# Layer 0 of a four-layer Flamingo stack: rope of the context in place on VectorE, attention in nine turns, routing in twelve parts

## The chip, the cores and the metric

The kernel runs on one core of a Trainium2 chip. The metric is the device time of one execution in microseconds (us); lower is better. A core has a TensorE (PE in the profile), a VectorE (DVE), a ScalarE (ACT), a GpSimd (POOL) and a SyncE (SP), which here only issues transfers. All of them run their own instructions in order and wait for each other through semaphores; 16 DMA engines move data.

## The reference, cut to what matters

There are 16 sequences of 56 tokens of width 256 (896 tokens), and for each a context of 1500 rows of width 64. Four layers follow each other, each a gated cross attention and a gated feed-forward part, both on the normalised x and added to x:

```python
# layer 0: x is (16, 56, 256), ctx is (16, 1500, 64)
x = x + tanh(g_xattn[0]) * mha(norm(x), ctx)   # 16 heads of 16; token i sees the context's rows 0 to i, so 56 at most
x = x + tanh(g_ffn[0])   * moe(norm(x))        # 16 routed experts, top 4, and 2 shared experts
# layers 1 to 3: attention over all 1500 rows of the context
#   keys  = ctx * cos + rotate_half(ctx) * sin            # "rope", the same for each of the three layers
#   x = x + tanh(g) * attention(norm(x), keys); then a matrix in fp8 (layer 1) or routed experts (2, 3)
```

The rope of the context (16 x 1500 x 64 numbers) depends on nothing that layer 0 makes. It is needed first by layer 1's attention.

## The kernel before, in words

The 896 tokens are eight tiles of 112 (`NT`, two sequences each). `x` stays in SBUF for the whole kernel, and so does `kv`, the roped context: 125 partitions, for each of the eight tiles 12 rows of the context x 2 sequences x 64 per partition. Layer 1 reads `kv` when it turns it into its keys.

Nearly every instruction is recorded with `in_order`, which keeps the order of the program on its engine. So the order that the code writes down is the order on each engine's queue, and a wait holds up all that stands behind it on that engine.

Layer 0's attention is `attention_mha`. First x, weights and the first 56 context rows (`k0`) are loaded, x is normalised (`norm`, L470 to L474), turned and multiplied with the query weights (L482 to L498). Then a loop of ten turns (`for i in range(NT + 2)`) works on three tiles at once. In turn i, tile i gets its scores (TensorE, L509 and L515), the shift by the row's maximum (VectorE, L529 and L530) and the exponential (ScalarE, L533); the weights of tile i-1 are turned (L540, L542), multiplied with the values (L549) and divided (L557, L558); and tile i-2's context is turned (L563, L565), projected (L570) and added to x (L573). At a turn's end the next tile's keys (L449, copied by ScalarE at L452 into `kb`) and values (L458, copied at L463 into `vb`) are made.

Between these steps `route(i, phase)` advances the routing. `Router.token_tiles` is a generator for a batch of two tiles: statistics (L1034), the inverse root (L131 to L141), the normalised rows (L1040), their transposes (L1048) and the product with the router weights (L1056), softmax (L1059 to L1065), the rank of every expert by comparing all pairs (L1069 to L1073), the choice and running totals (L1074 to L1081), the rows' places (L1091 to L1102), and eight indirect transfers by POOL that scatter the rows into `rows` in DRAM (L1106). Its `yield`s cut it into nine parts. Two of the four batches are left over at the loop's end; `moe` finishes them (`before`, `last`), and writes the table of tiles (`r.table()`) and the first products of the shared experts (`now`, L1414, then L1425 to L1433) between them.

`rows` must be cleared ahead of the scatters: `clear_rows` issues 16 transfers of zeros from SP (L1162).

Rope is the class `Roping`. `load` brings one tile's context from DRAM into `raw` (two buffers, SP, L874), and `parts` makes the rope on GpSimd: raw times cos into `kv` (L880), then for each half raw times sin into `rot` and an addition (L885, L886). Tiles 0 to 3 are roped in the first four turns, tiles 4 to 7 in parts between the routed tiles; the loads of tiles 6 and 7 are issued when these begin.

The routed tiles (`tiles` in `moe`) are 34 tiles of up to 128 rows of one expert, with nine spare ones that run only when needed. For each, SP loads weights and rows three tiles ahead (L1197, L1198, L1204); TensorE turns the rows (L1211), multiplies (L1223), turns the product (L1234) and multiplies again (L1245); ScalarE has the activation (L1227), VectorE the multiplication with it (`act`, L1228), a copy (`hT`, L1236) and the addresses (`to`, L1215); POOL scatters the result (L1248). `during(i)` adds work after each tile: the second half of the shared experts after every fourth, rope after every second.

Of the kernel before, what the change touches and what calls it, by code (L numbers as in the profile page):

```python
# [36 lines left out]
F32 = mybir.dt.float32  # L37
# [9 lines left out]
L, DC = 1500, 64  # L47
# [27 lines left out]
def flamingo_kernel(ctx: ExitStack, tc: tile.TileContext, d: dict, out: bass.AP):  # L75
# [72 lines left out]
    def inverse_root_now(pool, var, n):  # L148
        root = inverse_root(pool, var, n)
        while True:  # L150
            try:
                next(root)
            except StopIteration as e:
                return e.value
# [225 lines left out]
    def attention_mha(router, roping):  # L380
        with ExitStack() as st:
# [18 lines left out]
            def load_k0(b, queue):  # L400
                in_order(queue.dma_start(k0[S * b : S * b + S], d["ctx"][:, 0:S, :].rearrange("(t b) s c -> b s t c", b=2)[b]))
# [12 lines left out]
            kb = ap1.tile([128, 4, 2, 4, S], F32, name="kb")  # L414
# [6 lines left out]
            in_order(nc.gpsimd.memset(kb, 0.0))  # L421
            in_order(nc.gpsimd.tensor_copy(identb, ident))
            in_order(nc.gpsimd.tensor_copy(maskb, bcast(mask, 1, 8)))
            in_order(nc.gpsimd.memset(qT[:, :, B * S :], 0.0))

# [5 lines left out]
            for t in range(2):  # L431
                roping.load(t, nc.sync)
# [12 lines left out]

            def keys(t):
                ps = ps_k.tile([128, 512], F32, name="k_ps")[:, 0 : 4 * TP].rearrange("p (q n) -> p q n", q=4)
                for q in range(4):
                    in_order(nc.tensor.matmul(ps[:, q, :], wk[:, q, :], k0d[:, 2 * t : 2 * t + 2, 0, :], start=True, stop=True))  # L449
                for h in range(4):  # L450
                    i = ps[32 * h : 32 * h + 32].rearrange("p q (b s) -> p q b s", b=2)
                    in_order(nc.scalar.copy(kb[32 * h : 32 * h + 32, :, :, h, :], i))  # L452

            def make_values(t):
                vb = vbs[t % 2]
# [5 lines left out]
                pv = ps.rearrange("p (b g a c) -> p b g a c", b=2, g=H // 2, a=2)  # L461
                for a in range(2):
                    in_order(nc.scalar.activation(vb[:, :, :, 16 * a : 16 * a + 16], pv[:, :, :, a, :], AF.Copy, scale=small[0:TP, C_M + a : C_M + a + 1]))  # L463
                return vb
# [35 lines left out]
            class Pair:  # L500
# [3 lines left out]
                def scores(self):  # L504
                    t = self.t
                    self.s = []
                    for u in range(2):
# [4 lines left out]
                        for q in (2 * u, 2 * u + 1):  # L512
                            for b in range(2):
# [4 lines left out]
                                    kb[:, q, b].rearrange("p h s -> p (h s)"),  # L518
# [16 lines left out]
                def turned(self):  # L535
                    self.pT = ap.tile([TP, H // 2, 128], F32, name="pT0")
                    for u in range(2):
# [3 lines left out]
                        copy = nc.scalar.copy if u == 0 else nc.vector.tensor_copy  # L541
                        in_order(copy(self.pT[:, 4 * u : 4 * u + 4, :], ps))  # L542

                def values(self):

                    self.c = misc()
                    for g in range(H // 2):
                        for b in range(2):
                            in_order(nc.tensor.matmul(  # L549
                                self.c[64 * b : 64 * b + 64, 34 * g : 34 * g + 34], self.pT[:, g, 64 * b : 64 * b + 64], self.vb[:, b, g], start=True, stop=True  # L550
# [28 lines left out]
            def route(i, phase):  # L579

                k = i - 4 - "abc".index(phase)
                if k >= 0 and k % 2 == 0 and k // 2 < len(batches):
                    next(batches[k // 2])
# [7 lines left out]
            pairs[0].vb = make_values(0)  # L591
            norm(0)
            turn_normed(0)
            queries(0)
            norm(1)
            in_order(nc.scalar.activation(gates, gates, AF.Tanh))
            for i in range(NT + 2):
                new, turn, last = at(i), at(i - 1), at(i - 2)
                if turn:
                    turn.turned()  # L600
                if last:
                    last.turn_context()
                route(i, "a")
                if new:
                    new.scores()
                route(i, "b")
                route(i, "c")
# [3 lines left out]
                route(i, "b")  # L611
                if turn:
                    turn.values()
                if last:
                    last.project()
                if turn:
                    turn.normalize()
                if last:
                    last.add()
# [3 lines left out]
                if i + 1 < NT:  # L623
                    keys(i + 1)
                    pairs[i + 1].vb = make_values(i + 1)
                route(i, "c")
                route(i, "a")
                route(i, "b")
                route(i, "a")
                route(i, "b")  # L630
                if i < 4:
                    roping.rope(i)
                    roping.load(i + 2, nc.sync)
                    for _ in range(5):
                        next(clear, None)
# [227 lines left out]
    class Roping:  # L863
        def __init__(self, pool):
            self.pool, self.raw = pool, {}
            self.cos = pool.tile([KP, KC, DC], F32, name="cos")
            self.sin = pool.tile([KP, KC, DC], F32, name="sin")

        def load(self, t, queue, pool=None):
            if t == 0:  # L870
                in_order(queue.dma_start(self.cos, d["cos_k"]))
                in_order(queue.dma_start(self.sin, d["sin_k"]))
            self.raw[t] = (pool or self.pool).tile([KP, 2, KC, DC], F32, name="raw", bufs=2)
            in_order(queue.dma_start(self.raw[t], d["ctx"][2 * t : 2 * t + 2].rearrange("b (p c) e -> p b c e", c=KC)))  # L874

        def parts(self, t):
            hd = DC // 2
            raw = self.raw.pop(t)
            o = kv[:, t].rearrange("p c b e -> p b c e")
            in_order(nc.gpsimd.tensor_tensor(o, raw, bcast(self.cos, 1, 2), ALU.mult))  # L880
            yield
            for h in range(2):
# [837 lines left out]
```

## Time and profile before

| | |
|---|---|
| time, median of 3 runs | 2383.44 us (2382.97 to 2384.99) |
| profiled execution: time, span | 2402.98 us, 2401.2 us |
| TensorE, VectorE, ScalarE, GpSimd busy | 94%, 64%, 51%, 17% of the span |
| attention's first scores (L509) | start at 22.32 us |
| turned weights of tiles 0, 1, 2 (L540) | start at 34.97, 41.45, 49.10 us |
| last addition of attention (L573) | starts at 140.65 us |
| first rows of routed tiles turned (L1211) | starts at 183.83 us |
| layer 1's attention, first steps on POOL (L746) | starts at 393.41 us |

A line of a view in order of time has the start, the length, engine, line of the kernel, operation, output and inputs, shapes, and in brackets how long the engine sat idle before it and who ended that wait. L703 is line 703 of the kernel; DMA in brackets is a transfer. POOL and SP show the issue of a transfer, not its length.

### The profile page before, as it was taken

What the parts mean: (1) busy time and instruction counts of PE and PEld (TensorE: products, weight loads), DVE (VectorE), ACT (ScalarE), POOL (GpSimd) and SP (SyncE); (2) the same over time, 40 slices, a digit from 0 to 9 for tenths busy, and PEclk for the clock granted to TensorE, in tenths of its full rate; (3) what the DMA queues carried; (4) which work ended last, traced back from release to release, by engine and by line L of the source; (5) the groups of instructions that cost most, each with busy time, mean ns of one, the idle gap of its engine ahead of it and who ended that gap; (6) DMA issues with size and microseconds to landing.
All of it is one profiled execution on the core that took longest, in us unless ns stands there. A gap on an engine that the chain in (4) does not pass through costs nothing. (4 is left out here: it accounts for less than half of the span.)

```text
span 2401.2 us, 47945 instructions
## 1 busy us (share of the span) xinstructions
PE 2248.3 (94%) x17853; PEld 1613.1 (67%) x17858; DVE 1532.0 (64%) x3546; ACT 1232.0 (51%) x2703; POOL 416.3 (17%) x715
## 2 busy tenths in 40 slices
PE   8668889999999999999999999979899999999697
PEld 5445665777777775447777777745577777777454
DVE  4752245778777777667777777624577777776222
ACT  4312335666666663346666666513566666665131
POOL 5445710000000002420000000001001111101233
PEclk9769999999999999989999999989899999999799
DMA  7726762000000002200000000054101000000596
GB/s 217 225 80 184 215 169 78 22 21 22 21 22 21 21 24 68 61 21 22 23 24 21 13 23 24 10 200 157 32 22 30 29 30 16 28 24 21 153 284 206
DMA packets 116676, 172.98 MB, mean 72 GB/s; under 512 B 20154, under 2 KB 78531, under 8 KB 115412
## 3 DMA queue, kind: packets, MB, share of 16 engines
q1 hardware_dynamic: 106902, 151.35, 20.9%
q0 software_dynamic: 7600, 17.14, 2.2%
q8 instruction: 144, 2.36, 0.4%
q10 hardware_dynamic: 1934, 1.34, 0.2%
q14 instruction: 96, 0.79, 0.1%
HBM read 131.24 MB, written 40.48 MB: 72 GB/s over the span
## 5 line engine op out<-in xcount | busy, mean ns | idle before, releaser
L726 ACT ACTIVATE p<-s_ps,nm 128x500 f32<-128x500 f32 x504 | 335.7, 675 | 364.7 <-DVE nm L717 364.7
L703 PE MATMUL s_ps<-kvT,qT 64*128 64x500 f32 x2016 | 487.5, 610 | 9.9 <-ACT p L735 4.1
L777 PEld LDWEIGHTS m_ps<-pT,kv 125*64 125x64 f32 x8064 | 436.7, 137 | 65.8 <-issue 57.1
L777 PE MATMUL m_ps<-pT,kv 125*64 125x128 f32 x8064 | 477.3, 275 | 1.8 <-ACT pT L770 1.2
L715 DVE TENSOR_REDUCE part<-s_ps 128x1 f32<-128x500 f32 x504 | 340.6, 678 | 216.3 <-PE s_ps L703 215.9
L703 PEld LDWEIGHTS s_ps<-kvT,qT 64*128 64x128 f32 x2016 | 186.7, 190 | 198.1 <-issue 123.8
L765 PE MATMUL m_ps<-ident,p 128*125 128x128 f32 x2016 | 298.3, 283 | 0.4
L720 DVE TENSOR_REDUCE nm<-s_ps 128x1 f32<-128x1500 f32 x168 | 287.2, 1710 | 2.2 <-PE s_ps L703 2.2
L765 PEld LDWEIGHTS m_ps<-ident,p 128*125 128x125 f32 x2016 | 248.2, 188 | 35.9 <-issue 26.1
L735 ACT ACTIVATE p<-s_ps,nm 128x1500 f32<-128x1500 f32 x168 | 254.9, 1517 | 0.8 <-DVE nm L720 0.8
L765 PE MATMUL s_ps<-ident,p 128*125 128x128 f32 x2016 | 249.9, 274 | 0.0
L746 POOL TENSOR_TENSOR den<-den 128x1 f32<-128x1 f32 x168 | 32.9, 196 | 1212.0 <-ACT p L726 1211.8
L765 PEld LDWEIGHTS s_ps<-ident,p 128*125 128x125 f32 x2016 | 234.9, 189 | 0.9 <-ACT p L726 0.2
L770 ACT COPY pT<-s_ps 125x512 f32<-125x512 f32 x336 | 181.0, 596 | 98.5 <-PE s_ps L765 82.8
L770 ACT COPY pT<-m_ps 125x512 f32<-125x512 f32 x336 | 185.3, 617 | 0.2
L1223 PE MATMUL gu_ps<-wgu,xT 128*128 128x448 f32 (+2 forms) x344 | 145.8, 552 | 23.2 <-DMA wgu<-in_L_wgu 14.6
L788 DVE TENSOR_TENSOR ctxT<-m_ps,rep 64x128 f32<-64x128 f32 (+1 forms) x384 | 104.4, 272 | 90.0 <-PE m_ps L777 78.6
L1228 DVE TENSOR_TENSOR act<-gu_ps,act 128x224 f32<-128x224 f32 (+2 forms) x78 | 31.3, 401 | 201.2 <-ACT act L1227 185.2
L768 DVE COPY pT<-m_ps 125x512 f32<-125x512 f32 x168 | 116.2, 692 | 10.0 <-PE s_ps L765 0.9
L312 ACT COPY qT<-q_ps 64x224 f32<-64x224 f32 x128 | 71.8, 561 | 97.2 <-PE q_ps L356 60.4
L1223 PEld LDWEIGHTS gu_ps<-wgu,xT 128*128 128x128 f32 x344 | 64.5, 198 | 76.5 <-issue 35.7
L768 DVE COPY pT<-s_ps 125x512 f32<-125x512 f32 x168 | 114.4, 681 | 0.0
(293 smaller groups left out, 2605.9 us busy)
## 6 DMA issues: line engine op xcount, KB each, us to landing
wgu<-in_L_wgu SPq DMA_DIRECT2D x36, 448.0 KB
rows<-zero SPq DMA_DIRECT2D x16, 899.5 KB
kvT<-turned_kv SPq DMA_DIRECT2D x16, 750.0 KB
wgu<-in_L_wgu SPq DMA_DIRECT2D x34, 352.0 KB
rep<-through SPq DMA_DIRECT2D x336, 32.0 KB
xrow<-rows SPq DMA_DIRECT2D x78, 128.5 KB
wgu<-in_L_wgu SPq DMA_DIRECT2D x8, 1024.0 KB
wd<-in_L_wd SPq DMA_DIRECT2D x36, 224.0 KB
```

The source lines that it names most:

```text
L312: nc.scalar.copy(o, i)
L703: in_order(nc.tensor.matmul(o[:, 0 : 4 * KP], qT[64 * b : 64 * b + 64, t, j * QT : (j + 1) * QT], kvTs[t][64 * b : 64 * b + 64, z * 4 * KP ...
L715: in_order(nc.vector.tensor_reduce(self.part[:, z : z + 1], sp0[z][:, 0 : 4 * KP], AX.X, ALU.max))
L720: in_order(nc.vector.tensor_reduce(self.nm[1], sp1[:, :, 0 : 4 * KP], AX.XY, ALU.max, negate=True))
L726: in_order(nc.scalar.activation(self.p[0][:, 4 * z * KP : 4 * (z + 1) * KP], sp0[z][:, 0 : 4 * KP], AF.Exp, bias=self.nm[0], accum_out=sel ...
L735: in_order(nc.scalar.activation(self.p[1].rearrange("p (z c) -> p z c", z=3), sp1[:, :, 0 : 4 * KP], AF.Exp, bias=self.nm[1], accum_out=se ...
L765: in_order(nc.tensor.transpose(ps[:, c, :], self.p[b][:, k : k + KP], ident))
L768: in_order(nc.vector.tensor_copy(o, ps))
L770: in_order(nc.scalar.copy(o, ps))
L777: in_order(nc.tensor.matmul(self.pv[64 * b : 64 * b + 64, :], kv[:, self.t, c, b, :], self.pT[:, c, b, :], start=c == 0, stop=c == KC - 1))
L788: in_order(nc.vector.tensor_tensor(ctxs[self.t][64 * a : 64 * a + 64, b, lo - 448 * a : hi - 448 * a], self.pv[64 * b : 64 * b + 64, cols] ...
L1223: in_order(nc.tensor.matmul(ps[:, s, 0:n], xT[:, k, :], wgu[:, k, s * n : (s + 1) * n], start=k == 0, stop=k == 1))
```

## The change

Rope moves to VectorE, in place. The context is loaded straight into `kv`, in an order that the host arranges (`ctx` as tile, partition, row, sequence, column; the first 56 rows a second time as `keys0`). All eight loads are issued by SP in turns 2 to 5 of the attention, behind all the clears; cos and sin come in turn 2. Between routed tiles `during` takes two parts of rope after each tile: for each of the eight context tiles two products with sin into `rot`, two products with cos in place, two additions, 48 parts in all.

The attention loop has nine turns: what was done two turns after the scores is done one turn after them, behind the values of the same tile. The matmuls of keys and values and their copies are separate functions now (`keys` and `keep_keys`, `make_values` and `keep_values`), keys are made two tiles ahead into one of two `kb` buffers, and the copies stand ahead of the scores. Routing begins in turn 2 and a batch has twelve parts. After the loop, `r.table()` stands behind the last part of the last batch.

```diff
-            kb = ap1.tile([128, 4, 2, 4, S], F32, name="kb")
+            kbs = [ap1.tile([128, 4, 2, 4, S], F32, name=f"kb{i}") for i in range(2)]
...
+            in_order(nc.gpsimd.memset(kbs[1], 0.0))
...
-            for t in range(2):
-                roping.load(t, nc.sync)
             clear = clear_rows(ap1)
...
-            def route(i, phase):
-
-                k = i - 4 - "abc".index(phase)
-                if k >= 0 and k % 2 == 0 and k // 2 < len(batches):
-                    next(batches[k // 2])
+            def route(i, *phases):
+
+                for k in phases:
+                    if (i - k) % 2 == 0 and 0 <= (i - k) // 2 < len(batches):
+                        next(batches[(i - k) // 2])
...
-            for i in range(NT + 2):
-                new, turn, last = at(i), at(i - 1), at(i - 2)
...
+            for i in range(NT + 1):
+                new, cur = at(i), at(i - 1)
+                if cur:
+                    cur.turned()
+                route(i, 2, 3, 5)
+                if cur:
+                    cur.keep_turned()
+                if i + 1 < NT:
+                    keep_keys(i + 1)
+                if new:
+                    keep_values(i)
+                route(i, 4)
                 if new:
                     new.scores()
...
+                route(i, 3, 4)
                 if new:
                     new.shift()
                     new.exps()
...
+                if cur:
+                    cur.values()
+                route(i, 5)
+                if cur:
+                    cur.normalize()
+                if i + 2 < NT:
+                    keys(i + 2)
+                if cur:
+                    cur.turn_context()
+                if i + 1 < NT:
+                    make_values(i + 1)
+                route(i, 5, 3, 4, 4)
+                if cur:
+                    cur.project()
+                    cur.add()
+                route(i, 3)
...
-                if i < 4:
-                    roping.rope(i)
-                    roping.load(i + 2, nc.sync)
-                    for _ in range(5):
-                        next(clear, None)
+                for _ in range(5):
+                    next(clear, None)
+                if i == 2:
+                    roping.load_tables(nc.sync)
+                if 2 <= i < 6:
+                    roping.load(2 * i - 4, nc.sync)
+                    roping.load(2 * i - 3, nc.sync)
...
     class Roping:
...
+        def load(self, t, queue):
+            in_order(queue.dma_start(kv[:, t], d["ctx"][t]))
+
+        def parts(self):
+
             hd = DC // 2
...
+            for t in range(NT):
+                for h in range(2):
+                    mine, other = slice(h * hd, (h + 1) * hd), slice((1 - h) * hd, (2 - h) * hd)
+                    in_order(nc.vector.tensor_tensor(
+                        self.rot[:, :, :, mine], kv[:, t, :, :, other], bcast(self.sin[:, :, mine], 2, 2), ALU.mult
+                    ))
+                    yield
+                for c in (slice(0, KC // 2), slice(KC // 2, KC)):
+                    in_order(nc.vector.tensor_tensor(kv[:, t, c], kv[:, t, c], bcast(self.cos[:, c], 2, 2), ALU.mult))
+                    yield
+                for c in (slice(0, KC // 2), slice(KC // 2, KC)):
+                    in_order(nc.vector.tensor_tensor(kv[:, t, c], kv[:, t, c], self.rot[:, c], ALU.add))
+                    yield
...
                 before, last = tail
                 next(last)
+                next(before)
+                next(last)
+                next(before)
                 now[0][0]()
                 next(before)
+                for _ in range(4):
+                    next(last)
+                now[1][0]()
+                for _ in range(3):
+                    next(last)
...
                 next(last)
                 next(last)
...
                 r.table()
...
-                if i % 2 == 0 and rest:
+                if rest:
+                    next(rest, None)
                     next(rest, None)
...
-        "ctx": i["ctx_512"],
+
+        "ctx": i["ctx_512"].reshape(NT, 2, KP, KC, DC).transpose(0, 2, 3, 1, 4),
+        "keys0": i["ctx_512"].reshape(NT, 2, L, DC)[:, :, 0:S].transpose(1, 2, 0, 3),
```

## The prediction

> **What bounds the kernel now.** I read the page first (TensorE busy 94% of a span of 2401.2 us; the chain that ended last covers the end only), and then the stretch the change touches, by windows of 20 us and by engine in order of time. Everything from layer 1's attention on (after about 390 us) is untouched and only shifts, so the question is when layer 0's routed tiles start and how fast they run.
>
> ```profile
> 40.00:60.00 20.00, 19.80 (x190) 14.13 (x191) 11.01 (x24) 13.72 (x27) 9.07 (x6) 1.00 0.83 235
> 120.00:140.00 20.00, 10.64 (x68) 8.49 (x68) 11.37 (x41) 2.44 (x6) 5.63 (x6) 0.59 0.10 30
> 200.00:220.00 20.00, 18.70 (x74) 11.73 (x73) 4.66 (x16) 6.40 (x17) 15.24 (x11) 0.95 0.73 207
> ```
> Columns: length, then PE, PEld, DVE, ACT, POOL busy, granted clock, DMA share, GB/s. TensorE fills the first attention turns (19.8 of 20) and the routed tiles (18.7); between, at 120 to 140, it works 10.6 us at a clock of 0.59. That middle is a chain of waits:
>
> ```profile
> 71.49 0.98 PE L1048 MATMUL m_ps<-ident,xr 112*128 112x112 f32 x4 [7.28 <-DVE xr L1040]
> ...
> 94.11 0.93 PE L1091 MATMUL m_ps<-sel,small 112*112 112x16 f32 x4 [8.13 <-DVE sel L1074]
> ...
> 165.92 7.17 PE L1431 MATMUL sy_ps<-swd,shT 88*112 88x256 f32 x16 [2.89 <-DVE shT L1426]
> ...
> 183.83 0.38 PE L1211 MATMUL m_ps<-ident,xrow 128*128 128x128 f32 x2
> ...
> 196.23 0.66 PE L1211 MATMUL m_ps<-ident,xrow 128*128 128x128 f32 x2 [5.41 <-DMA xrow<-rows]
> ```
> The routed tiles start at 183.83 and stall 5.41 us at the fourth, whose rows queue behind two context loads that SP issues at 179.35. The two waits for VectorE come from GpSimd's rope:
>
> ```profile
> 81.27 2.95 DVE L1065 TENSOR_TENSOR p<-p,sum_p 112x32 f32<-112x32 f32 x1
> 84.26 2.25 DVE L1069 TENSOR_TENSOR eq<-p 112x512 f32<-112x512 f32 x1
> ...
> 154.10 0.19 DVE L1065 TENSOR_TENSOR p<-p,sum_p 112x32 f32<-112x32 f32 x1
> 154.32 0.69 DVE L1069 TENSOR_TENSOR eq<-p 112x512 f32<-112x512 f32 x1
> ```
> While rope runs on GpSimd (80.72 to 92.5) the operations with two inputs from SBUF take 2.2 to 2.9 us, later 0.69 and 0.19. From 81.27 to rank at 93.16 that is 11.9 us against 2.9 at 154.10 to 156.98: 9.0 lost. The root at 62.94 takes 8.0 instead of 2.5: 5.5 lost.
>
> Last, the DMA, by fine slices of 15 to 40 us (0.625 us each), and two issues of SP:
>
> ```profile
> DMA  3389996333333333333333999966999999999899
> GB/s 120 128 315 386 376 348 212 128 123 123 123 128 123 121 118 123 123 123 118 118 118 123 340 338 337 349 209 215 340 344 334 255 237 270 253 291 258 222 262 240
> ```
> ```profile
> 109.74 0.33 SPq L231 DMA_DIRECT2D wkr<-in_L_wkr  x1
> ...
> 113.22 0.42 SPq L1398 DMA_DIRECT2D swgu<-in_L_wgu  x1
> ```
> In the threes (19.4 to 28.8, the first two context loads) a third of the 16 DMA engines works, at about 121 GB/s; in the nines (the clears) all, at about 345. A context load of 768,000 bytes costs the queue 6.3 us, a clear of 921,088 bytes 2.7. SP's queue stays full until about 118 us: at 109.74 it goes on only when a context load has landed.
>
> **The change part by part.** The sum is made against the profiled execution (span 2401.2, time 2402.98), which stands 0.8% above the median of 2383.44; I take the difference over to the median.
>
> *Rope off GpSimd.* 8 tiles of 3.49 + 4 x 1.84 = 10.9 us leave POOL (87 us). Half of it ran beside attention and cost VectorE the 14.5 us above; those are gone. In the routed tiles POOL waits for y anyway, so no further gain there.
>
> *Rope on VectorE.* 48 operations of 768 elements per partition, two after each of 24 routed tiles. The nearest rows are 112x512 at 0.69 and 112x32 at 0.19, so 1.04 ns an element: 0.96 us each, about 0.9 in sequence, 1.8 a tile. A tile needs VectorE for act 0.34, hT 0.41, to 0.20 (0.8 in sequence, e.g. 237.96 to 238.75): 2.6 in all. TensorE needs 2.49 a tile back to back (233.73, 236.22, 238.71), but four tiles take 13.5 (229.44 to 242.94), since one carries shared work (1.7) and one waits 1.2 for weights; VectorE needs 4 x 2.6 + 1 = 11.4. The cover is there, 2 us in four tiles, and act has about 1.1 us before the next transposes ask for it, against a lag of 0.1 to 0.2 a tile. I take 2 us in all (ends 0 and 12; if the cover is gone the full cost is 43).
> Here a rule has to be weighed. The rows say that VectorE waits behind GpSimd's rope. The Trainium skill ("SBUF — State Buffer", Who interferes with whom) says that a VectorE instruction with two SBUF inputs and a GpSimd instruction that reads SBUF exclude each other for the whole instruction. POOL's scatter of results comes once a tile: were it to block rope as rope blocked VectorE, each pair would cost up to 1 us more, 24 in all. But the 0.69 of 154.32 was measured while POOL issued scatters (152.12 to 162.03), and the page infers the same: descriptors need the write side, which tensor_tensor leaves alone. I take nothing for it. The diag products on POOL do read SBUF, but rope ends at tile 23, where they begin.
>
> *Nine turns.* A turn without routing is bound by TensorE, 7.5 us (41.45, 49.10, 56.62), and has the same matmuls after; score, values and projection of one tile now meet within two turns instead of three. A batch brings VectorE 11.6 us, a pair of turns 8.6: 10.1 a turn, beside 10.0 and 11.8 measured at the two turns that rope left alone (72.26 to 82.29, 107.15 to 118.93). Before, routing begins in turn 4; now in turn 2, a batch cut into twelve parts instead of nine. ScalarE's copies of keys (2.17) and values (0.84) now precede a turn's exps; those were ready for it only 2 to 3 us later (53.56 to 54.22), so they fill that wait. So: turn 3 starts at 49 as before, five turns of 10.5 give 101.5, the last 8.5: TensorE reaches the shared experts' first product at about 112, where before it was at 140.41. Nothing new waits in the loop: kb has two buffers, sloti and xr are reused a full two turns later (scatters of a batch take 10 us). The loop alone would gain 28.
>
> *Context loads.* All eight now go ahead of the shared experts' weights on SP; before, six did. They keep 125 partitions. The Trainium skill ("DMA: Bandwidth & Descriptors", Why a DMA increments its semaphore by 16 and not by 1) says a DMA is spread over the largest number up to 16 that divides the outermost size of both sides: 5 for 125, which is the third of the trace. Longer contiguous rows (6144 bytes instead of 3072) thus buy no engines. This rule speaks against the change: with it eight loads cost 51 us; at the clears' rate they would cost 18.
> The queue: the first clear goes at about 12 (zero's memset waits for one more memset of 1.6); 16 clears 43 us, to 55; tables 6.3, to 61; six contexts 38, to 99; weights for layer 1 (1.9 MB) 5.5, scatters of two batches 5.2, two contexts 12.6, to 122; with landing and SP's wait for an older load some 3 more: 125. By difference: 116 (113.22 and landing) + 12.6 for two loads + 2.6 for one batch more - 6.1 of SP's waits for POOL's buffers = 125. So the shared weights land 13 us after TensorE asks (ends 112 and 132), and in its order stand the last batch's transposes behind that product. What the loop gains beyond that is lost here.
>
> *Tail.* From 125, with before's durations at its slow clock: product 4.9, transposes and copy 1.6, logits 1.6, top and exp 0.8, VectorE to rank and totals 4.6, which the second product (5.6) slightly exceeds, places 1.8, to sloti 1.5 and weight 0.6, table 4.1, shT 0.5: 147. Then the shared work that took 17.9 before (165.92 to 183.83): routed tiles start at 165. The last scatters, now ahead of the table instead of behind it, end at 152, rows land at 156, so they don't wait. Gain 19.
>
> *Two context loads gone from the head of the routed tiles*: 5.4, and about 1 for the clock after that stall.
>
> Sum: 19 + 6.4 - 2 = 23. 2383.4 - 23 = 2360. k0 in rows of 2 KB instead of 256 bytes may bring x a microsecond or two earlier; the DMA queue sets the end there, so nothing is counted.
>
> **The rivals.**
> 1. The shared weights are there in time (kv rows run faster, or loads overlap with other queue work on the idle 11 engines). Then the 112 of the loop holds: gain 32 + 6 - 2 = 36, 2347. For: 11 engines stand idle in the threes. Against: SP waited at 109.74.
> 2. Rope shows in the tiles, half a microsecond in each of 24: 12 less, 2372. For: 2.6 against TensorE's 2.49 back to back. Against: the four-tile period of 13.5.
> 3. Slower: rope's operations are blocked as those of 84.26 were, at 2.25 each, because POOL has a scatter in every tile. VectorE would need 5.3 a tile against 3.4: 1.9 x 24 = 46 lost, net 23 slower, 2406. It decides from about 1.9 us an operation. Against: 154.32.
> 4. The change doesn't do what it says, since the queue's end moves as much later as rope's stall brings: swgu at 145 or later. It would need the loads at 75 GB/s. About 2383.
>
> **How the numbers follow.** Forecast (weights late, 2353 to 2366) 0.53; rival 1 0.2; rival 2 0.18; rival 4 0.04; rival 3 0.05. The likeliest is 2360. From 2343 (rival 1 with a few us from the clock) to 2376 (rival 2 with the queue at 132) nearly nine in ten are held; what is cut off are rivals 3 and 4 and the tails. Within 0.2% (4.8 us, about what a measurement of this kernel can tell from no change): 0.04; slower 0.06; faster 0.90.
>
> **What would show it.** Right: VectorE's eq and gt at 0.69 in every batch; TensorE idle over 8 us before the shared experts' first product, with DMA swgu as releaser; routed tiles from about 165, no stall at the fourth; rope at 0.9 to 1.0 us, the pace of four tiles still 13.5. Wrong: no wait for swgu (rival 1); act or hT as releaser of TensorE in the tiles (2); rope over 1.9 us (3).

## The result, and the profile after

The changed kernel takes 2376.25 us (median of 20 runs, 2369.95 to 2382.74); the kernel before takes 2388.53 (20 runs beside them). The ratio is 0.9956, 95% interval 0.9947 to 0.9964: some 11 us faster by the ratio, 12.3 between the medians, where 23 were forecast. With the runs of the later experiments it was measured again: 2371.2 against 2390.06, ratio 0.9928 (0.9915 to 0.994). The two intervals do not meet, so the gain is 10 to 17 us, depending on the set of runs. One of before's 20 runs took 3187.47 us, which its median hardly feels. The profiled execution of the changed kernel took 2372.64 us, span 2370.8.

TensorE in the profile of after (the changed kernel), in order of time (start, length, what; in brackets the wait and its releaser):

```profile
115.19 0.53 PE L1106 MATMUL m_ps<-sel,small 112*112 112x16 f32 x2 [1.90 <-DVE sel L1092]
141.04 5.80 PE L1429 MATMUL sgu_ps<-xnT,swgu 128*88 128x448 f32 x8 [24.21 <-DMA swgu<-in_L_wgu]
...
160.96 7.17 PE L1446 MATMUL sy_ps<-swd,shT 88*112 88x256 f32 x16 [0.88 <-DVE shT L1441]
...
179.09 0.38 PE L1226 MATMUL m_ps<-ident,xrow 128*128 128x128 f32 x2
...
185.92 0.38 PE L1226 MATMUL m_ps<-ident,xrow 128*128 128x128 f32 x2
```

TensorE is through with the routing of the loop at 116.8 us, and then does nothing for 24.21 us until the shared experts' weights land. The routed tiles start at 179.09 (before 183.83, forecast 165). The fourth tile (185.92) no longer waits for rows. In windows of 20 us (length, then PE, PEld, DVE, ACT, POOL busy, granted clock, DMA share, GB/s):

```profile
40.00:60.00 20.00, 19.06 (x203) 13.97 (x199) 13.61 (x40) 11.78 (x23) 0.00 (x0) 1.00 1.10 252
120.00:140.00 20.00, 0.00 (x0) 0.00 (x0) 0.41 (x2) 0.00 (x0) 6.86 (x9) 0.50 0.66 208
200.00:220.00 20.00, 17.69 (x77) 12.07 (x77) 15.24 (x30) 6.23 (x17) 8.21 (x7) 1.00 0.79 235
```

GpSimd (fifth pair) is empty in the loop where it had 9.07 us. From 120 to 140 not one matmul runs. In the routed tiles VectorE has gone from 4.66 to 15.24 us, and TensorE is about as full as before (17.69 us at a clock of 1.00, before 18.70 at 0.95). Why the weights are late stands in SP's row of issues and in the DMA by slices of 0.625 us from 60 to 85 us:

```profile
10.29 52.29 SPq L1177 DMA_DIRECT2D rows<-zero  x16
...
66.01 17.70 SPq L893 DMA_DIRECT2D kv<-in_ctx  x6
83.76 14.27 SPq L233 DMA_DIRECT2D wqr<-in_L_wqr  x1
...
121.75 0.81 SPq L893 DMA_DIRECT2D kv<-in_ctx  x2
122.68 0.35 SPq L1413 DMA_DIRECT2D swgu<-in_L_wgu  x1
```

```profile
DMA  9999999999999997877533342333233235546464
GB/s 214 273 240 199 224 298 250 235 222 230 255 260 242 222 215 200 225 258 253 192 146 136 123 154 108 128 138 133 113 147 138 118 138 194 189 164 248 154 227 171
```

The clears fill all engines until about 71 us: 14.7 MB from 10.3 us on, 3.8 us each at some 243 GB/s. Only then come cos, sin and the contexts, on a third of the engines at about 130 GB/s. SP is held for 14.27 us at 83.76 behind them and passes the last two contexts at 121.75. So `swgu`, the shared experts' weights, is issued only at 122.68, when TensorE has been ready for 5.9 us, and lands behind these two contexts, at 141.

VectorE's own rows are as forecast:

```profile
67.93 0.69 DVE L1083 TENSOR_TENSOR eq<-p 112x512 f32<-112x512 f32 x1
...
182.16 1.82 DVE L901 TENSOR_TENSOR rot<-kv,sin 125x768 f32<-125x768 f32 x2
183.91 0.34 DVE L1243 TENSOR_TENSOR act<-gu_ps,act 128x176 f32<-128x176 f32 x1
184.16 0.41 DVE L1251 COPY hT<-m_ps 88x256 f32<-88x256 f32 x1
```

The pairwise comparison takes 0.69 us in every batch (0.75 in one), and two parts of rope fit between a tile's own operations in 1.82 us.

### The profile page after: what moved, and what is told of

It is laid out like the page before. It is cut to its first block, busy times and chain, and to the rows that moved or that the text cites. A ratio compares the mean times of both kernels' runs of the same rounds, so it can differ in the third digit from the quotient of the medians.

```text
span 2370.8 us, 47911 instructions
## 1 busy us (share of the span) xinstructions
PE 2226.7 (94%) x17853; PEld 1603.2 (68%) x17858; DVE 1556.8 (66%) x3594; ACT 1232.3 (52%) x2703; POOL 342.8 (14%) x676
## 5 line engine op out<-in xcount | busy, mean ns | idle before, releaser
L1263 POOL DMA_INDIRECT results<-y,to x78 | 90.6, 1162 | 203.5 <-ACT y L1262 193.8
```

The lines of the kernel that those rows point to most:

```text
L1263: i = nc.gpsimd.indirect_dma_start(flat, bass.IndirectOffsetOnAxis(ap=to[:, 0:1], axis=0), y, None, bounds_check=B * S * top - 1, oob_is_e ...
```

## The experiments

Each was timed in five rounds beside the kernel before; ratios are to that, the intervals are 95%.

### Is it the queue? Three reliefs, and the change once more

**Contexts in two transfers**, so that the large one's partitions can be dealt to 15 engines:

```
-    in_order(queue.dma_start(kv[:, t], d["ctx"][t]))
+    for part in (slice(0, 120), slice(120, KP)):
+        in_order(queue.dma_start(kv[part, t], d["ctx"][t][part]))
```

> Each context goes as two transfers, partitions 0 to 119 and 120 to 124. Theory (the DMA queue sets when the shared experts' weights land, and a context over 125 partitions runs on 5 of 16 engines): the 120 partitions go over 15 engines, a context takes 2.4 to 3.2 us of the queue instead of 6.15, eight save some 25 us, the weights land near 116 us instead of 141, TensorE's own readiness at 116.8 becomes the bound, and the routed tiles start near 155 instead of 179: 20 to 25 us faster than the changed kernel, 2351 to 2356. Rival A (the queue is held by something else, its rate from memory or the number of transfers in flight): the weights land within 5 us of 141 and the time moves by less than 5 us, or is worse for having twice the transfers. Rival B (the loop before it sets the end, the weights only seem late): no change.

Measured: 2364.1, ratio 0.9893 (0.9872 to 0.9914). The DMA slices from 60 to 85 us, and TensorE:

```profile
DMA  9889999989989889998779899794532334975999
GB/s 234 230 215 201 187 276 254 287 274 257 226 197 167 128 177 246 211 226 187 172 143 197 197 261 236 172 241 113 154 147 88 138 138 158 294 187 159 311 236 285
```

```profile
125.06 5.48 PE L1430 MATMUL sgu_ps<-xnT,swgu 128*88 128x448 f32 x8
...
162.63 0.38 PE L1227 MATMUL m_ps<-ident,xrow 128*128 128x128 f32 x2
```

The engines stay mostly busy through the contexts, TensorE meets no wait for weights, and the routed tiles start 16.5 us earlier than in the first profile of the change. Part of this is not the split's doing: here the 16 clears were issued in 44.80 us instead of 52.29, and against the change's second profile below, whose clears ran alike, it is 8.8 us. TensorE is through with the loop not at 116.8 but at 125.1, with two stalls taken up below; so the time fell by 7 to 15 us and not by 20 to 25.

**Contexts 6 and 7 behind the shared experts' weights:**

```
-    if 2 <= i < 6:
+    if 2 <= i < 5:
         roping.load(2 * i - 4, nc.sync)
 ...
     sh = Shared(pool, ps_h, ps_o, side)
+    for t in (6, 7):
+        rest.__self__.load(t, nc.sync)
```

> Contexts 6 and 7 are issued just behind the shared experts' weights on SP instead of just ahead of them. Theory (weights stand behind the contexts): the weights land two contexts earlier, 12.3 us, near 129; the routed tiles start near 167: 12 us faster than the changed kernel, 2364. The two contexts land near 143, ahead of the rows of the routed tiles, so no stall comes back at the fourth tile. Rival (the queue is bound by total bytes before the routed tiles and what is moved behind returns as a late row or weight load): less than 4 us gain, with a stall of 5 us at a first routed tile.

Measured: 2364.21, ratio 0.9897 (0.988 to 0.9913).

```profile
124.48 5.49 PE L1431 MATMUL sgu_ps<-xnT,swgu 128*88 128x448 f32 x8
...
162.12 0.38 PE L1226 MATMUL m_ps<-ident,xrow 128*128 128x128 f32 x2
```

No wait for weights, no stall at the fourth tile: nothing comes back behind. That the tiles start at 162 and not at 167 goes with the clears, issued in 45.33 us here too.

**Clears from a wider source**, each partition's seven rows in one piece:

```
-    zero = pool.tile([128, DX], F32, name="zero")
+    zero = pool.tile([128, CT, DX], F32, name="zero")
 ...
-    in_order(nc.sync.dma_start(rows[e * CT : (e + 1) * CT].rearrange("c p x -> p c x"), bcast(zero, 1, CT)))
+    in_order(nc.sync.dma_start(rows[e * CT : (e + 1) * CT].rearrange("c p x -> (c p x)").rearrange("(p c x) -> p c x", p=128, x=DX), zero))
```

> The changed kernel, with the clears written from a wider source, seven rows (7,196 bytes) in one piece for each partition instead of rows of 1,028 bytes; the bytes are the same. Theory (the clears' packets are the limit: 52 ns for 1,028 bytes is 20 bytes a ns, a context's 235 ns for 6,144 bytes is 26): 16 clears take at most 45 us of the queue instead of 54 to 62, the shared experts' weights land 10 to 17 us earlier, at 124 to 131, and the time falls by 8 to 12 us to 2364 to 2368. Rival (the memory's write rate is the limit, 245 to 290 GB/s whatever the pieces): no change in the clears' end, less than 2 us in time.

Measured: 2366.67, ratio 0.9891 (0.9875 to 0.9908). The DMA from 10 to 50 us in slices of 1 us:

```profile
DMA  5559999899999999999999999999999999999833
GB/s 126 172 237 453 389 417 446 367 453 403 403 446 403 410 417 410 426 396 410 453 396 410 439 403 419 403 396 425 403 410 446 396 417 439 381 432 396 302 105 152
```

The clears run at some 410 GB/s and end at about 48 us instead of 71: 2.3 us each. So the memory was not what held them to 243 to 285 GB/s; it was how they were cut, pieces of 1,028 bytes with one source row sent seven times. The edit changes the piece and the source together, and no run separates the two. The first product starts at 126.56 without a wait.

**The changed kernel once more**, beside the last of these runs:

> The changed kernel once more, on the chip of these runs. What it tells apart: its first profile had clears at 3.84 us each and no stall of TensorE in the values' products, the split and the late-context kernels had clears at 3.4 and stalls of 5 to 7 us twice. If these belong to the kernels, clears at 3.8 come back and no stalls; if they differ from run to run, clears at 3.4 and the stalls appear here too, the weights land at about 134 instead of 141, and the time lies within 3 us of 2376.

Measured: 2371.2, ratio 0.9928 (0.9915 to 0.994).

```profile
10.31 45.10 SPq L1177 DMA_DIRECT2D rows<-zero  x16
```

```profile
134.09 5.34 PE L1429 MATMUL sgu_ps<-xnT,swgu 128*88 128x448 f32 x8 [10.28 <-DMA swgu<-in_L_wgu]
```

The clears' rate differs between two profiled executions of one kernel (45.10 us of issues instead of 52.29), and with it the weights' landing, 134 instead of 141. Why is open: the later runs were made on several chips, and none separates the chip from chance. The stalls that the first profile did not have appear. The time was 5 us under the first median, more than expected.

The three reliefs touch three different transfers and give the same time, 2364 to 2367, and no wait for weights. That the weights stood behind too much queue work is shown. Once they do not, TensorE is bound by the loop and the part behind it.

### Which half of the change brought the gain

**Nine turns alone**: the changed loop, with rope, loads and first keys of the kernel before (the loop's lines for `roping` and `clear`, `Roping`, `during`, `ctx` and `k0` as before):

> Nine turns with routing in twelve parts alone: rope stays on GpSimd, in the loop for four tiles and in the routed tiles for four, with the loads, layouts and first keys of the kernel before. Theory (the queue decides): the weights stand behind six contexts, not eight, and land near 120 to 128, earlier than in the changed kernel; TensorE is ready for them some 10 us later than 116.8, since GpSimd's rope blocks VectorE; so the routed tiles start near 167 to 172, with the stall of 5.4 us at the fourth: 12 to 17 us faster than before, that is about the same as the changed kernel or a few us better. Rival (the gain of the changed kernel comes from rope's leaving GpSimd): less than 5 us faster than before.

Measured: 2390.09 against 2390.91, ratio 1.0002 (0.9988 to 1.0015): no gain at all, and the first of the two theories is wrong as it stood. VectorE, and then TensorE:

```profile
77.58 3.22 DVE L1087 TENSOR_TENSOR p<-p,sum_p 112x32 f32<-112x32 f32 x1
80.83 2.23 DVE L1091 TENSOR_TENSOR eq<-p 112x512 f32<-112x512 f32 x1
```

```profile
144.85 5.61 PE L1437 MATMUL sgu_ps<-xnT,swgu 128*88 128x448 f32 x8
...
182.63 0.38 PE L1234 MATMUL m_ps<-ident,xrow 128*128 128x128 f32 x2
...
193.72 0.41 PE L1234 MATMUL m_ps<-ident,xrow 128*128 128x128 f32 x2 [4.10 <-DMA xrow<-rows]
```

The weights are there in time, but the first product comes later than before's (140.41): GpSimd's rope blocks VectorE in the new order too, 3.22 and 2.23 us instead of 0.19 and 0.69. What the loop loses, 4.4 us, the part behind it regains: from the first product to the routed tiles it takes 37.8 us, before 43.4.

**Rope on VectorE alone**, in the loop of ten turns, loads at before's places (`Roping`, `during` and the inputs as in the change, not shown):

```
     if i < 4:
-        roping.rope(i)
         roping.load(i + 2, nc.sync)
 ...
-    rest = rest(st)
-    next(rest)
+    for t in (6, 7):
+        rest.__self__.load(t, nc.sync)
+    rest = rest()
```

> Rope on VectorE between the routed tiles alone, with the contexts loaded straight to where they stay and the first keys in longer rows; the loop of ten turns, the routing in nine parts and the places of the eight context loads (six in the loop between the clears, two at the head of the routed tiles) stay as in the kernel before. Turns alone gave no change (0.9998 to 1). Theory (the two halves need each other: turns gain nothing while GpSimd's rope blocks VectorE, and rope's leaving gains at most those 14.5 us, of which the loop's own order returns part): 4 to 10 us faster than before, 2380 to 2386, so less than the whole change. Rival (rope's leaving is the whole gain): 11 to 13 us faster, as the changed kernel; then the nine turns bring nothing at all.

Measured: 2375.78 against 2390.06, ratio 0.9939 (0.9924 to 0.9954): the whole gain or nearly, as the rival said.

```profile
125.31 4.92 PE L1408 MATMUL sgu_ps<-xnT,swgu 128*88 128x448 f32 x8
...
168.61 0.38 PE L1203 MATMUL m_ps<-ident,xrow 128*128 128x128 f32 x2
...
180.19 0.66 PE L1203 MATMUL m_ps<-ident,xrow 128*128 128x128 f32 x2 [4.58 <-DMA xrow<-rows]
```

The first product comes 15.1 us earlier than before's 140.41, and the routed tiles start earlier than in the changed kernel. The stall at the fourth tile is still there.

**Ten turns with contexts 6 and 7 behind the weights** instead of at the head of the tiles (the two lines of the late-context kernel, in the kernel of rope alone):

> Rope on VectorE with the loop of ten turns and nine parts, as in the rope-alone kernel, but with contexts 6 and 7 issued just behind the shared experts' weights instead of at the head of the routed tiles. Against the late-context kernel it differs in the loop (and the places of the first six contexts) alone, so it prices the nine turns with the queue out of the way. Theory (nine turns are worth some 6 us at the start of the routed tiles, 168.6 against 162.1, and the stall of 4.6 us at the fourth tile goes with the loads): routed tiles start near 168, no stall, 4 to 5 us faster than rope alone: ratio 0.992, 2371, some 6 us slower than the late-context kernel. Rival (nine turns bring nothing, all that differed was the stall): the same time as the late-context kernel, ratio 0.9897, 2365.

Measured: 2370.39, ratio 0.9916 (0.9894 to 0.9938).

```profile
126.50 5.24 PE L1408 MATMUL sgu_ps<-xnT,swgu 128*88 128x448 f32 x8
...
170.14 0.38 PE L1203 MATMUL m_ps<-ident,xrow 128*128 128x128 f32 x2
```

Against the late-context kernel (0.9897) nine turns are worth some 4.5 us, but the two intervals overlap. The profiles say where it would come from: the first product is only 2.0 us later (126.50 against 124.48), but from it to the routed tiles ten turns take 43.6 us and nine 37.6 (170.14 less 126.50, 162.12 less 124.48). It is the part behind the loop that is shorter, as with the turns alone, not the loop. Whether the finer cut of a batch does this, or the new order behind the loop, no run separates.

### Is rope covered in the routed tiles?

**Without rope** (it is left out: the generator's six parts per tile only yield):

> Leaves out rope: kv keeps the raw contexts, the 48 VectorE operations between the routed tiles are gone, everything else stays. Theory (rope is covered, since the pace of the tiles after the sixth was the same with it as without): within 2 us of the changed kernel, and the scatters of results fall from 1.77 to about 1.0 us without moving the time. Rival (rope costs half a microsecond in each of 24 tiles): 10 to 12 us faster than the changed kernel, 2365.

Measured: 2413.02, and not comparable as a whole: with unroped keys the later layers route otherwise, and the kernel runs 17,985 matmuls instead of 17,853. Up to layer 0's end the work is the same, so the pace of the tiles is read there, from the sixth to the twenty-second tile:

```profile
185.09 0.38 PE L1215 MATMUL m_ps<-ident,xrow 128*128 128x128 f32 x2
...
241.23 0.38 PE L1215 MATMUL m_ps<-ident,xrow 128*128 128x128 f32 x2
```

That is 56.1 us without rope, 55.9 and 54.9 with it (the change's two profiles, 193.91 to 249.84 and 186.26 to 241.16) and 56.8 before (207.04 to 263.81). Half a microsecond a tile, as rival 2 had it, would be 8 us over these sixteen. Rope is free there. The scatters of results take 0.97 us in this kernel, as expected.

### Why the loop does not end at 112

In the split kernel VectorE waits 5.66 us for the last tile's products with the values, long after TensorE has run them (111.50 to 113.43), while GpSimd issues scatters of rows (106.10 to 115.73). In the line, `remote` means that the profile names no releaser:

```profile
117.68 0.26 DVE L569 RECIPROCAL den<-m_ps 128x16 f32<-128x16 f32 x1 [5.66 <-remote]
```

**The second batch's scatters after the loop**, in the split kernel (they are kept in a function and called behind the loop):

> The split kernel (contexts in 120 and 5 partitions), with the eight scatters of the second routing batch issued after the loop instead of within its last turns. Theory (scatters that GpSimd issues while TensorE does a tile's products with the values hold both up: 5.1 us before the last project in the split kernel): that stall is gone, TensorE is ready for the shared experts' first product near 119 instead of 123.6, and the later scatters still end ahead of the table: 3 to 5 us faster than the split kernel. Rival (the stall has another cause, or the scatters, now later, become the bound of the rows): the stall stays or the first rows come late, and the time is the split kernel's or up to 5 us worse.

Measured: 2363.36, ratio 0.9893 (0.9878 to 0.9907), and it tested nothing: on GpSimd nothing stood ahead of the scatters, so they ran at 105.9 to 115.5 as ever. GpSimd's last of them, and VectorE:

```profile
114.56 0.94 POOL L1125 DMA_INDIRECT rows<-xr,sloti  x1 [0.30 <-issue]
```

```profile
117.40 0.26 DVE L569 RECIPROCAL den<-m_ps 128x16 f32<-128x16 f32 x1 [5.32 <-remote]
```

**A copy on GpSimd ahead of them** that reads the last tile's divided context, in the split kernel:

> The deferred kernel left the scatters of the second batch where they were in time (105.9 to 115.5 us: on GpSimd nothing stood ahead of them), so it tested nothing. Here a small copy on GpSimd, which reads the last tile's divided context, stands ahead of them, so they can't start before VectorE has passed the place where it waited 5.3 us. Theory (these scatters hold up the values' products or their signal to VectorE): the wait before the last division falls from 5.3 to under 1 us, TensorE is ready for the shared experts' first product near 119 instead of 123.6, routed tiles start near 158: 3 to 5 us faster than the split kernel, ratio near 0.9875. Rival (another cause): the wait of 5 us stays, scatters start at 118 and end 12 us later, and the time is that of the split kernel, or a few us worse.

Measured: 2364.09 against 2395.77, ratio 0.9873 (0.9847 to 0.9898). In GpSimd's order the copy came to stand behind seven of the eight:

```profile
117.18 0.93 POOL L1127 DMA_INDIRECT rows<-xr,sloti  x1 [0.30 <-issue]
```

```profile
119.90 0.26 DVE L569 RECIPROCAL den<-m_ps 128x16 f32<-128x16 f32 x1 [3.39 <-remote]
```

The wait is 1.9 us shorter, with one scatter fewer (1.24 us with its gap), and ends 1.8 us after the seventh (118.11), as it ended 1.9 us after the eighth (115.50) above.

**All eight behind the division**, in the split kernel: on GpSimd their places are added to zero times the last tile's divided context (`behind`).

```
+    zero = pool.tile([TP, 2 * top], F32, name="after_ctx")
+    in_order(nc.gpsimd.tensor_scalar(zero, behind, 0.0, None, ALU.mult))
+    at = pool.tile([TP, 2, top], I32, name="sloti_late")
 ...
+    in_order(nc.gpsimd.tensor_tensor(zero, slot, zero, ALU.add))
+    in_order(nc.gpsimd.tensor_copy(at, zero))
```

> In the waiting kernel only the last of the eight scatters of the second batch stood behind the copy; the wait before the last division fell with it from 5.3 to 3.4 us and ended 1.8 us after the seventh scatter. Here all eight stand behind the division: their places are added, on GpSimd, to zero times the last tile's divided context. Theory (VectorE gets the values' products only some 1.8 us after GpSimd's group of scatters has ended): the wait is gone, the division runs within 0.2 us of TensorE's last values' product, TensorE is ready for the shared experts' first product 4 to 5 us earlier than in the split kernel for the same start of the loop, and the scatters, now later, end at about 143 us instead of 150 or a few us later, so that the rows are just in time: 2 to 5 us faster than the split kernel, ratio 0.987 to 0.9885. Rival (the link with the scatters is chance): a wait of 5 us stays at the division, and the time is the same or worse.

Measured: 2363.49 against 2392.11, ratio 0.9877 (0.9859 to 0.9895).

```profile
114.17 0.26 DVE L569 RECIPROCAL den<-m_ps 128x16 f32<-128x16 f32 x1 [1.45 <-PE m_ps L561]
```

```profile
116.45 1.15 POOL L1133 DMA_INDIRECT rows<-xr,sloti_late  x1 [0.28 <-POOL sloti_late L1130]
```

The division follows TensorE at once, 5.2 us after the last turning of weights (109.01) where the split kernel took 9.4 (108.32 to 117.68): 4.2 us of stall went with the scatters. The first shared product starts at 121.72 instead of 125.06. The time is not resolved from the split kernel's, and VectorE shows where the gain went:

```profile
128.23 0.73 DVE L1056 TENSOR_SCALAR xr<-x,mv,y 112x256 f32<-112x256 f32 x2 [3.61 <-DMA rows<-xr,sloti_late]
```

The last batch's rows reuse the buffer that the delayed scatters read, so they wait for these 3.61 us and come at 128.23 (split kernel 128.05); the routed tiles start at 163.29. The stall became a wait for a buffer.

### Everything at once

**Contexts split, clears wide, contexts 6 and 7 late:**

> Nine turns, rope on VectorE, and all three reliefs of the queue at once: contexts in 120 and 5 partitions, clears in pieces of 7,196 bytes, contexts 6 and 7 behind the shared experts' weights. Theory (with any one of them the loop is the bound already, TensorE being ready at 122 to 125 us and the weights there before): no better than each alone, ratio 0.989 to 0.990, 2363 to 2366, routed tiles from 162 to 164. Rival (the queue still slows the loop through what it holds up, so relief adds): routed tiles start before 158 and the ratio is below 0.987.

Measured: 2362.24, ratio 0.9886 (0.9863 to 0.9908), as the theory had it for the time; the place was wrong. The loop itself ended later in the profiled execution:

```profile
130.73 5.96 PE L1432 MATMUL sgu_ps<-xnT,swgu 128*88 128x448 f32 x8
...
169.04 0.38 PE L1227 MATMUL m_ps<-ident,xrow 128*128 128x128 f32 x2
```

Some of that is the granted clock of this one execution. From 62 to 66 us TensorE is busy throughout in the split kernel and in this one, at a clock of 1.00 there (first line) and of 0.50 here (second):

```profile
62.00:66.00 4.00, 4.00 (x61) 2.99 (x59) 2.98 (x7) 3.44 (x8) 0.00 (x0) 1.00 1.04 254
62.00:66.00 4.00, 4.00 (x12) 2.53 (x12) 1.14 (x4) 0.09 (x1) 0.00 (x0) 0.50 0.46 142
```

The turn from the third tile's products with the values to the fourth's takes 12.9 us here (58.06 to 70.94), 9.6 in the split kernel (55.48 to 65.10). Two more kernels whose clock fell to 0.5 to 0.6 there take 12.9 as well (the one without rope, 55.31 to 68.19, and the copy on GpSimd, 55.74 to 68.61). That is 3.3 us. Another 2.6 stand ahead of the first tile's products (42.57 against 39.99), most of which wide clears alone have too (41.74). Together they make up the 5.7 us by which the first product is later. So the late place says little; it is the times that say that relief does not add up. By the ratios this kernel and the split one beat both the kernel before (by 26 to 27 us) and the changed one (by 8 to 17, as its ratio of 0.9956 or 0.9928 is taken); among themselves the relieved kernels are not told apart.

## Why the prediction was wrong, step by step

*Rope off GpSimd: 14.5 us.* Right. Rope alone brings the first shared product from 140.41 to 125.31, 15.1 us, and the comparison takes 0.69 us in every batch.

*Rope on VectorE: 48 operations of 0.96, covered, 2 us in all.* Right: 0.946 each, 1.82 for two, and no cost in the pace of the tiles. Rivals 2 and 3 fall. One thing under it was wrong in the other direction. I held scatters and rope to leave each other alone, and cited the Trainium skill ("SBUF — State Buffer", Who interferes with whom) for its inference on descriptors. VectorE indeed is not held up (0.953 at most), but the scatter is: 1.77 us in most of the tiles with rope, 0.97 without it. It costs nothing here, since GpSimd waits for y anyway. What of the scatter waits, the writing of its descriptors or the reading of its addresses, no run separates.

*Nine turns: TensorE ready at 112, the loop alone gains 28.* Wrong in two ways. Alone they gain nothing (nine turns alone: 1.0002), since rope on GpSimd still blocks VectorE there; the 28 already held the 15 of rope. And with rope gone TensorE is ready at 116.8 in the first profile and 123.8 in the second. The terms as written give 110 (49, five turns of 10.5, 8.5), not 112. In the first profile turn 3 starts at 52.41, the five turns take 10.3 each, as forecast, and the last takes 12.8. In the second they start at 51.23 and take 11.2 each and 16.8, with the stall of 5.03 us behind a group of scatters in the last. None of this decided: the weights came later than that. From the first product to the routed tiles I took 40 us, and it is 38 and 37 in the change's two profiles and 43 with ten turns.

*The queue: weights land at 125.* This is the step that failed: the term of 16 clears at 2.7 us, 43 in all, to 55. They took 3.8 us each, to 71, in the first profile of the change and 3.4, to 64, in the second. I had read the rate from the best slices of before (about 345 GB/s). The 18 slices in the prediction's fence that follow the contexts have a mean of 283 GB/s (5094 by 18), which is 3.25 us each, and 9 us later for all behind: weights at 134, as the second profile has them. The further 7 us of the first profile lie in clears at a mean of 243 GB/s; why they were slower there is open. The rest of that step held: contexts at 6.1 us each (768,000 bytes at 125 GB/s), behind them the weights for layer 1, two contexts and swgu. So the weights landed at 141 and 134, which is 16 and 9 us after the forecast, by as much as the clears ended late. TensorE stood for 24.2 and 10.3 us instead of 13. The rule of the Trainium skill that spoke against the change ("DMA: Bandwidth & Descriptors", Why a DMA increments its semaphore by 16 and not by 1) was right about the contexts: 125 partitions a third of the engines, 120 nearly all.

*Tail and head of the tiles.* The stall of 5.4 us is gone. Before's routed tiles start at 183.83, the change's at 179.09 in the first profile and 171.44 in the second: a gain of 4.7 or 12.4 for the 19 of the sum. From there to the reading back of results before's tiles take 134.8 us, the change's 123.0 and 122.0: some 12 for the 4.4 of the sum. Half of that is before's profiled execution alone. It took 2402.98 us, 14 above its median, and nine turns alone, with the same rope and loads between the tiles, need 129.0 there (182.63 to 311.61). Against those the gain is 6 to 7 us. For the same reason the start of layer 1 is better compared with nine turns alone, whose time is before's: its first GpSimd sum starts at 385.49 there, in the change at 378.41 and 367.26, so 7 and 18 us earlier, beside gains of 11 and 17 in the times. The rest of the span, untouched by the change, took 1992 to 2008 us in the profiled executions of all these kernels (the one without rope aside), so a single profile says nothing more about the end.

So the mechanism was the forecast one, late weights, and one term of its sum was too small. Rival 4 (the queue's end moves as much later as rope's stall brings) came nearer than I had let it: its swgu at 145 is 4 us from what the first profile shows, at a chance of 0.04. I had tied it to loads at 75 GB/s. Twenty us more on eight loads would be 87, and the loads ran at 125 all the same: it was the clears that moved the end. By the profiles, what kept the change from rival 4's 2383 is the stall at the fourth tile and the few us behind the loop. The likeliest case and rival 4 differed in one term of the queue, whose bound I had not given from both sides.

## What to carry to other kernels

Where an order of transfers on one queue decides, take each one's rate as a mean over a whole stretch in which it runs, not from its best slices, and give the range from the worst stretch to the best. A change that moves loads ahead of something is to be priced at that something: three cheap reliefs (two loads later, 120 partitions and 5 instead of 125, pieces of 7 KB instead of 1 KB) each gave back the 7 to 15 us that the new order cost. And of two halves of a change, ask what each brings while the other's obstacle still stands: here turns alone brought nothing.

## What the runs showed of the hardware that was not expected

While GpSimd issues a group of eight scatters of rows, TensorE's small matmuls (the 32 products with the values, each 34 columns wide), or their signal to VectorE, are held up. Thirteen of the fourteen profiles show it wherever such products fell into a group. Either TensorE pauses between these products, 1.1 to 3.5 us in all, and starts the last of them 1.5 to 1.9 us after the group's last scatter. Or VectorE waits 3.4 to 6.0 us and starts the division 1.8 to 2.0 us after that scatter. So it is with rope alone, whose group ends at 101.68:

```profile
103.47 0.26 DVE L558 RECIPROCAL den<-m_ps 128x16 f32<-128x16 f32 x1 [6.00 <-PE t_ps L541]
```

Moving one group away removed the wait at its place. The first profile of the change is the exception: its products at 87.53 and 107.25 lie inside groups and nothing waits. What tells it apart is open, and so is the mechanism.

Most scatters of results take 1.77 us instead of 0.97 while VectorE runs operations with two inputs from SBUF beside them. And the clears in pieces of 1,028 bytes ran at 243 to 285 GB/s, in pieces of 7,196 bytes at 410.
